# A two-layer cross-attention and mixture-of-experts kernel: where the scatters, the keys, the first maxima and the clears of two tables stand in the order of work

## The chip, the cores and the metric

The program runs on one core of one Trainium2 chip. The metric is the device time of one execution in microseconds. Everything is computed in float32.

Five engines work side by side, each through its own queue of instructions: TensorE (PE, matrix products), VectorE (DVE), ScalarE (ACT), GpSimd (POOL) and SyncE (SP), which issues most of the DMAs. A DMA that goes to places given by a list of indices (a scatter or a gather) is issued by GpSimd.

## The reference

Four blocks are applied to x (4 batches of 512 tokens of 256 numbers). `ctx_1024` is a second input of 4 x 1601 rows.

```python
x = x + L0_xattn(ctx_1024, layernorm(x), ...)   # 8 heads of 128, keys: context and latents
x = x + L0_ffn(layernorm(x), ...)               # 8 experts, top 2, capacity 512
x = x + L1_xattn(ctx_1024, layernorm(x), ...)   # 8 heads of 32, 1601 keys from the context
x = x + L1_ffn(layernorm(x), ...)               # 8 experts, top 2, no capacity
```

In the first expert block every token goes to its two best experts. It gets a slot of the expert in the order of the tokens, and an expert has 512 slots:

```python
slot = where(offsets < capacity, bin_ids * capacity + offsets, E * capacity)
xb   = zeros((E * capacity + 1, hs)).at[slot].set(xf[src])
h    = gelu(einsum('ech,ehf->ecf', xb, w1))
y    = einsum('ecf,efh->ech', h, w2)
out  = zeros((T, hs)).at[src].add(flat_w[order][:, None] * yv)
```

The second attention is a softmax over 1601 keys for each of 8 heads: `softmax(q k^T * scale) v`. The second expert block has no limit to an expert's tokens, and it adds biases.

## The kernel before, in words

The program has four stages, one after the other: first attention (A), first experts (B), second attention (C), second experts (D). A planner in the language's compiler puts the instructions of each engine in order: it follows the program's order where it has a choice, and lets a later instruction go ahead where an earlier one isn't ready by its own reckoning. In some parts the program forbids that: `in_order(*computing)` keeps TensorE, VectorE, ScalarE and GpSimd in the written order (stage C from line 1572 on), and `keep_in_program_order` places one instruction behind the one that was written before it on its engine. SP's queue is not under `in_order` in stage C.

*Stage B.* `route` (three steps: `normalize`, `choose`, `send`) finds the slots of one batch, and `send` (line 308) writes the batch's rows to the DRAM table `slot_x` with 8 scatters. Batches 0 to 2 are routed during stage A, batch 3 in stage B. `all_experts(half, beside)` (line 1222) runs the eight experts on one half of their 512 slots, 256 rows at a time: `fetched` loads the rows from `slot_x` (line 1175) and the expert's two weights of 1 MB each (lines 1178, 1179), `turned` transposes the rows, `hidden` is the first layer with its gelu, `results` the second layer and the store to `slot_y` (line 1220). Row and weight tiles have two buffers each. The first half needs only rows of batches 0 to 2 in the usual case: between the halves, `tc.If(again > 0)` (line 1286) repeats the first half where that did not hold.

`beside` is a generator of other work that is stepped between the experts' pieces, twice for each expert. In the first half it is `keys_first` (line 1258): the routing of batch 3 with its scatters, then 15 steps of keys and values of the second attention for batch 0 (`keys_values`, line 998). In the second half it is `keys_next` (line 1295): the keys and values of batch 1, the collecting of batch 0's results (`add_collected`), its queries, the seven maxima of unit 0 and their way into a row (`negated`, `to_row`).

Also in stage B, four clears are issued with each expert: 8 DMAs fill the second halves of `slot_y` with zeros (line 1248), and 41 DMAs of 530 KB fill the tables `rows_a` and `rows_b` of the second expert block (line 393). Their source `empty` is one row of 265 numbers in each partition.

*Stage C.* The work is cut into 16 units (4 batches x 2 groups of 4 heads x 2 halves of the queries). A unit has 13 steps, one for each block of 128 keys: scores (`weights`, line 1387), exponential (line 1400), sum (line 1409), product with the values (line 1418). The exponential needs the largest score of each query first: `maxima(u, g)` (line 1113, with its reduction on VectorE in line 1124) computes it in 7 pieces, ahead of the unit. `negated` and `to_row` write it into a spare row of `asked`, the tile of the queries, and `keyed`, the tile of the keys, has ones in that row, so that the score comes out less its maximum. `keyed` has one tile for each group of heads. It is filled with zeros and the row of ones (lines 1364, 1365), and `load_keys` (line 1367) brings the keys to their places with 4 DMAs. Both are done at the start of stage C for both tiles, and the first three pieces of unit 1's maxima follow (line 1575). Other work is given a step of the order by `put(step, ...)` (line 1520); the gathers of the next batch's results are put at steps 1 to 8 and their sums at steps 14 to 20, and `load_queries` of unit u at step 13u - 12.

*Stage D* reads `rows_a` and `rows_b`, which the routing in stage C fills.

Of the kernel before, what the change touches and what calls it, by code (L numbers as in the profile page):

```python
# [74 lines left out]
def xattn_ffn_twice(ctx: ExitStack, tc: tile.TileContext, a: dict, out: bass.AP):  # L75
# [267 lines left out]
    def add_collected(b, got, tiles=range(NT)):  # L343
        for t in tiles:
            for k in range(2):
                j = b * NT + t
                xs = x[b][:, t, :]
                nc.vector.scalar_tensor_tensor(
                    xs, got[2 * t + k], prob[k][:, j : j + 1], xs, ALU.mult, ALU.add
                )  # L350
# [31 lines left out]
        nc.sync.dma_start(rbias, a["br"].partition_broadcast(P))  # L382
        nc.sync.dma_start(b2, a["b2"])

    def clear_rows(empty):

        for rows in (rows_a, rows_b):
            n = rows.shape[0]
            for i in range(0, n, 4 * P):
                some = rows[i : min(i + 4 * P, n), :]  # L390

                tc.keep_in_program_order(
                    nc.sync.dma_start(
                        some.rearrange("(p r) d -> p r d", p=P),
                        empty.unsqueeze(1).to_broadcast([P, some.shape[0] // P, PAY]),
                    )
                )
                yield

    def route2(b, two, psum, tag, first=0, n=NT):  # L400

# [651 lines left out]
    for t in shift + asked:  # L1053
        nc.vector.memset(t, 0.0)

    def queries(b, qT):
        xn = soon.tile([P, NT, D], F32, tag="xn", name="xn")
        mv = ln_moments(turns, x[b], NT)
        root = ln_root(turns, mv, NT)
        yield  # L1060
        mv, rs = ln_scale(turns, mv, NT, root)
        for i in range(NT):
            ln_apply(xn, x[b], mv, rs, i)
        yield
        xnT = soon.tile([P, DC, S], F32, tag="xnT", name="xnT")
        transposed(banks["s"], "s", xnT, xn, NT)
        yield
        for o in range(DC):
            ps = banks["s"].tile([P, 512], F32, tag="s", name="ps_q1")
            for c in range(DC):  # L1070
                nc.tensor.matmul(
                    ps,
                    lhsT=wT[:, 0, c, o * P : (o + 1) * P],
                    rhs=xnT[:, c, :],
                    start=c == 0,
                    stop=c == DC - 1,
                )
            nc.scalar.activation(qT[:, o, :], ps, AF.Copy, scale=DH1**-0.5)
            yield

    units = [(b, o, f) for b in range(B) for o in range(DC) for f in range(2)]
    qTs = {}

# [76 lines left out]
    with ExitStack() as st:  # L1160
# [8 lines left out]
        def slots(of, e, half):  # L1169
            s0 = e * CAP + half * HALF  # L1170
            return of[s0 : s0 + HALF, :].rearrange("(t p) d -> p t d", p=P)
# [10 lines left out]
        def turned(e, half, sx, w1, w2):  # L1182
            sxT = two.tile([P, DC, HALF], F32, tag="xT", name="sxT")
            tp = ps_t.tile([P, DC, CT, P], F32, tag="m", name="tp_x")
            for c in range(DC):
                for t in range(CT):
                    nc.tensor.transpose(tp[:, c, t, :], sx[:, t, c * P : (c + 1) * P], ident)
            nc.vector.tensor_copy(sxT, tp.rearrange("p c t q -> p c (t q)"))
            return e, half, sxT, w1, w2
# [32 lines left out]
        def all_experts(half, beside):  # L1222

            here = turned(*fetched(0, half))
            last = None
            for e in range(E):
                done = hidden(*here)
                next(beside, None)
                for _ in range(4):
                    next(clear, None)  # L1230
                if e + 1 < E:
                    here = turned(*fetched(e + 1, half))
                if last:
                    results(*last)
                next(beside, None)
                last = done
            results(*last)
            assert next(beside, None) is None

        empty = rt.tile([P, PAY], F32, name="empty")  # L1240
        nc.gpsimd.memset(empty, 0.0)
        nc.gpsimd.memset(empty[:, D : D + 1], NOWHERE)

        def clears():

            for e in range(E):
                tc.keep_in_program_order(
                    nc.sync.dma_start(
                        slots(slot_y, e, 1), empty[:, :D].unsqueeze(1).to_broadcast([P, CT, D])
                    )  # L1250
                )
                yield
            yield from clear_rows(empty)

        clear = clears()
        kvs = []

        def keys_first():
            normalize()
            yield  # L1260
            choose()
            send()
            yield
            *kv, steps = keys_values(ps_s, "s", 0)
            kvs.append(kv)
            for k, f in enumerate(steps):
                f()
                if k % 2:
                    yield

        normalize, choose, send = route(B - 1, rt, soon, ps_t, "m")
        all_experts(0, keys_first())
# [22 lines left out]
        def keys_next():  # L1295
            *kv, steps = keys_values(ps_s, "s", 1)
            kvs.append(kv)
            for f in steps[:6]:
                f()
            yield  # L1300
            add_collected(0, got0)
            for k, f in enumerate(steps[6:]):
                f()
                if k % 3 == 2:
                    yield
            begin(0)
            for _ in queries(0, qTs[0]):
                yield
            load_queries(0)
            for g in range(len(pieces)):  # L1310
                maxima(0, g)
                yield
            negated(0)
            to_row(0)

        all_experts(1, keys_next())
        assert next(clear, None) is None


    def turned_rows(rows, xT, tp):  # L1320
# [29 lines left out]
    with ExitStack() as st:  # L1350
# [5 lines left out]
        ps_m = st.enter_context(tc.tile_pool(name="c_ps_m", bufs=1, space=PSUM))  # L1356
        banks.update(s=ps_s, m=ps_m)

        keyed = [one.tile([P, 2, M], F32, name=f"keyed{o}") for o in range(DC)]
        of_ones = ones[:, 0:1].to_broadcast([P, M])
        for t in keyed:
            nc.scalar.activation(t[:, 0], of_ones, AF.Copy, scale=in_row[:, 0:1])
            nc.vector.tensor_scalar(t[:, 1], of_ones, in_row[:, 0:1], None, ALU.mult)

        def load_keys(b, o):
            for pair in range(2):
                for s in range(2):
                    i = 2 * pair + s  # L1370
                    nc.sync.dma_start(
                        keyed[o][64 * s : 64 * s + 32, pair, :],
                        kvs[b][0][o][i * DH1 : (i + 1) * DH1, :],
                    )


        by_pool = (1, 4, 7, 10)
# [188 lines left out]

        put(NM * n_units + 2, lambda: first_layer(range(0, FC // 2, 2)))
        put(NM * n_units + 5, lambda: first_layer(range(FC // 2, FC, 2)))

        load_keys(0, 0)  # L1570
        load_keys(0, 1)
        ordered = st.enter_context(in_order(*computing))

        for g in range(3):
            maxima(1, g)
        ahead = {}
        for u in range(1, n_units):
            for g in range(len(pieces)):
# [441 lines left out]
```

## Time and profile before

| | us |
|---|---|
| median of 3 runs | 2905.28 |
| lowest, highest | 2904.32, 2910.24 |
| the profiled execution, its own time | 2910.62 |
| its span, first to last instruction | 2908.8 |
| TensorE busy in the span | 2746.4 (94%) |
| VectorE, ScalarE, GpSimd busy | 1460.5, 935.3, 379.8 |
| TensorE busy, 1546 to 1932 us (stage B and the end of A) | 348.9 of 386 |
| TensorE busy, 1932 to 2604 us (stage C) | 596.0 of 672 |

TensorE is the busiest engine in every stage, so a share below the full one in a stage says how much of that stage is waiting. Busy time in stretches is read with the column of the granted clock beside it (1.00 is the full speed), because a matmul at half clock counts as busy for twice as long. A wait that is named after a DMA was ended by that DMA's landing. SP's queue has no busy time of its own; its lines show when DMAs are issued.

### The profile page before, as it was taken

What the parts mean: (1) busy time and instruction counts of PE and PEld (TensorE: products, weight loads), DVE (VectorE), ACT (ScalarE), POOL (GpSimd) and SP (SyncE); (2) the same over time, 40 slices, a digit from 0 to 9 for tenths busy, and PEclk for the clock granted to TensorE, in tenths of its full rate; (3) what the DMA queues carried; (4) which work ended last, traced back from release to release, by engine and by line L of the source; (5) the groups of instructions that cost most, each with busy time, mean ns of one, the idle gap of its engine ahead of it and who ended that gap; (6) DMA issues with size and microseconds to landing.
All of it is one profiled execution on the core that took longest, in us unless ns stands there. A gap on an engine that the chain in (4) does not pass through costs nothing. (4 is left out here: it accounts for less than half of the span.)

```text
span 2908.8 us, 36010 instructions
## 1 busy us (share of the span) xinstructions
PE 2746.4 (94%) x13614; PEld 1860.1 (64%) x13614; DVE 1460.5 (50%) x2339; ACT 935.3 (32%) x1325; POOL 379.8 (13%) x290
## 2 busy tenths in 40 slices
PE   6999999999999999999998799998989989799998
PEld 2666666766766667666666577864444454458887
DVE  6445556554476444554454302148876767763111
ACT  3323334332343223332332111124434434352221
POOL 0000000100001000000000101002223414152442
PEclk9999999999999999999999999999999999899999
DMA  5444343434344333333335698820001011106563
GB/s 164 111 113 114 97 110 92 109 93 99 89 111 107 97 89 93 97 92 102 95 97 150 197 241 238 236 72 23 23 12 61 24 38 35 39 31 223 161 214 99
DMA packets 196435, 311.96 MB, mean 107 GB/s; under 512 B 43319, under 2 KB 117368, under 8 KB 193560
## 3 DMA queue, kind: packets, MB, share of 16 engines
q1 hardware_dynamic: 157512, 227.52, 29.4%
q0 software_dynamic: 14160, 46.31, 5.4%
q10 hardware_dynamic: 24576, 35.68, 4.8%
q8 instruction: 112, 1.84, 0.3%
q14 instruction: 75, 0.61, 0.1%
HBM read 111.73 MB, written 51.34 MB: 56 GB/s over the span
## 5 line engine op out<-in xcount | busy, mean ns | idle before, releaser
L810 DVE TENSOR_REDUCE top<-ps_s 128x1 f32<-128x2113 f32 x128 | 301.8, 2358 | 581.7 <-PE ps_s L802 581.7
L839 PE MATMUL ps_o<-pT,v 128*128 128x256 f32 x2176 | 521.7, 381 | 0.5 <-DVE inv L817 0.5
L802 PE MATMUL ps_s<-kT,qT 128*128 128x512 f32 (+1 forms) x1280 | 489.0, 526 | 6.0 <-ACT attn L816 6.0
L839 PEld LDWEIGHTS ps_o<-pT,v 128*128 128x128 f32 x2176 | 410.0, 191 | 115.1 <-issue 68.4
L816 ACT ACTIVATE attn<-ps_s,top 128x2113 f32<-128x2113 f32 x128 | 259.0, 2024 | 476.4 <-DVE top L810 446.1
L802 PEld LDWEIGHTS ps_s<-kT,qT 128*128 128x128 f32 x1280 | 241.4, 190 | 252.8 <-issue 236.7
L831 DVE STREAM_TRANSPOSE pT<-swapped 128x2176 f32<-128x2176 f32 x128 | 312.4, 2441 | 33.6 <-DMA swapped<-attn 23.3
L1124 DVE TENSOR_REDUCE tops<-ps_s 128x2 f32<-128x1024 f32 (+1 forms) x224 | 238.0, 1105 | 152.0 <-PE ps_s L1113 151.6
L1387 PE MATMUL ps_w<-asked,keyed 64*128 64x256 f32 (+1 forms) x1664 | 247.4, 420 | 20.3 <-DVE tops L1124 9.5
L751 PE MATMUL ps_k<-kvin,wkv 128*128 128x512 f32 (+1 forms) x640 | 262.7, 533 | 3.3 <-DVE mv_g L689 1.7
L785 PE MATMUL ps_v<-wkv,kvin 128*128 128x256 f32 x1088 | 254.5, 381 | 1.4 <-ACT v L792 1.4
L1387 PEld LDWEIGHTS ps_w<-asked,keyed 64*128 64x128 f32 (+1 forms) x1664 | 149.0, 192 | 147.0 <-ACT pT L1400 61.6
L1400 ACT ACTIVATE pT<-ps_w 128x1024 f32<-128x1024 f32 (+1 forms) x176 | 179.5, 1024 | 195.2 <-PE ps_w L1387 191.8
L785 PEld LDWEIGHTS ps_v<-wkv,kvin 128*128 128x128 f32 x1088 | 204.8, 190 | 36.6 <-ACT v L792 5.9
L1409 DVE TENSOR_TENSOR sum<-sum,pT 128x1024 f32<-128x1024 f32 (+1 forms) x128 | 183.0, 1430 | 10.3 <-ACT pT L1400 4.0
L764 ACT ACTIVATE kT<-ps_k,bqk 128x512 f32<-128x512 f32 (+1 forms) x160 | 96.9, 620 | 266.1 <-PE ps_k L751 123.4
L1409 POOL TENSOR_TENSOR sum<-sum,pT 128x1024 f32<-128x1024 f32 x48 | 122.5, 2553 | 350.3 <-ACT pT L1400 350.1
L751 PEld LDWEIGHTS ps_k<-kvin,wkv 128*128 128x128 f32 x640 | 115.9, 191 | 77.3 <-issue 66.7
L1113 PE MATMUL ps_s<-kv,qT 32*128 32x512 f32 (+1 forms) x1024 | 135.9, 579 | 14.7 <-ACT kv L1017 6.5
L792 ACT COPY v<-ps_v 128x512 f32<-128x512 f32 x144 | 79.9, 561 | 216.7 <-PE ps_v L785 142.1
L1197 PE MATMUL ps_h<-sxT,w 128*128 128x256 f32 x512 | 118.6, 390 | 4.8 <-ACT hT L1204 4.1
L1211 PE MATMUL ps_y<-w,hT 128*128 128x256 f32 x512 | 114.5, 380 | 0.3 <-DVE y L1219 0.2
(300 smaller groups left out, 2662.8 us busy)
## 6 DMA issues: line engine op xcount, KB each, us to landing
swapped<-attn SPq DMA_DIRECT2D x1536, 68.0 KB, 2.0
swapped<-attn ACTq DMA_DIRECT2D x512, 68.0 KB, 2.2
w<-in_w_dram SPq DMA_DIRECT2D x32, 1024.0 KB, 6.2
rows_b<-empty SPq DMA_DIRECT2D x36, 530.0 KB, 14.3
w_e<-in_wall_dram SPq DMA_DIRECT2D x5, 2052.0 KB
cw<-in_ctxT_dram SPq DMA_DIRECT2D x4, 1601.0 KB, 6.4
keyed<-kv SPq DMA_DIRECT2D x32, 200.1 KB, 3.6
ctx_b<-in_ctx_dram SPq DMA_DIRECT2D x3, 1536.0 KB
```

The costliest lines, as they stand in the source:

```text
L751: nc.tensor.matmul(ps[:, :n], lhsT=wkv[:, c, hs], rhs=kvin[:, c, : NB - 1, k, :] if k < 4 else kvin[:, c, NB - 1, :, :], start=c == 0, sto ...
L785: nc.tensor.matmul(ps[:, k, :], lhsT=flat_kvin[c][:, j * P : (j + 1) * P], rhs=wkv[:, c, cols], start=c == 0, stop=c == DC - 1,)
L802: nc.tensor.matmul(flat[:, j0 : j0 + n], lhsT=qT[:, t * P : (t + 1) * P], rhs=kT[:, j0 : j0 + n], start=True, stop=True,)
L810: nc.vector.tensor_reduce(top, flat[:, :L], AX.X, ALU.max, negate=True)
L816: nc.scalar.activation(attn[:, :L], flat[:, :L], AF.Exp, bias=top, accum_out=total)
L831: nc.vector.transpose(pT[:, :, k * P : (k + 1) * P].rearrange("p c (a i) -> p a c i", a=4), swapped.rearrange("p a (c i) -> p a c i", i=32),)
L839: nc.tensor.matmul(ps, lhsT=v[:, j - parts[part][0], (h % 2) * DH0 : (h % 2 + 1) * DH0], rhs=pT[:, j, :], start=j == 0, stop=j == NB - 1,)
L1113: nc.tensor.matmul(pss[i // 2][:, i % 2, at : at + n], lhsT=qTs[b][rows, o, q0 : q0 + P], rhs=kvs[b][0][o][rows, j0 : j0 + n], start=True, ...
L1124: nc.vector.tensor_reduce(tops[u][:, t : t + at // n, 2 * pair : 2 * pair + 2, j0 // 512], of, AX.X, ALU.max,)
L1387: nc.tensor.matmul(ps[:r, s, pair * QH : (pair + 1) * QH], lhsT=keyed[o][64 * s : 64 * s + 64, pair, j * P : j * P + r], rhs=asked[u % 3][ ...
L1400: nc.scalar.activation(pT[:r], ps[:r], AF.Exp)
L1409: (nc.gpsimd if k else nc.vector).tensor_tensor(to, to, pT[:r], ALU.add)
```

## The change

1. `send` (the 8 scatters of batch 3) leaves the second step of `keys_first` and comes at its end, at the 21st call. The steps of keys and values are yielded one by one instead of in pairs, and empty steps are put in up to that call.
2. `beside` is stepped three times for each expert instead of twice.
3. The clears of `slot_y` stand one with each expert of the first half. The 41 clears of the rows leave stage B: each is put at a step of stage C, from step 2 on.
4. The first of the two `keyed` tiles is made in an earlier pool (`soon`), filled in the step of the scatters and loaded in the step after. The second is filled at step 4 of stage C and loaded at step 8. `empty` moves to the pool `soon` as well.
5. The first three pieces of unit 1's maxima move from the start of stage C to the end of `keys_next`, and `to_row(0)` stands after the first of them.

```diff
-    def clear_rows(empty):
+    def clear_rows():
+        def clear(some):
+            tc.keep_in_program_order(
+                nc.sync.dma_start(
+                    some.rearrange("(p r) d -> p r d", p=P),
+                    empty.unsqueeze(1).to_broadcast([P, some.shape[0] // P, PAY]),
+                )
+            )
         for rows in (rows_a, rows_b):
             n = rows.shape[0]
             for i in range(0, n, 4 * P):
...
-                yield
+                yield lambda some=rows[i : min(i + 4 * P, n), :]: clear(some)
...
+    keyed = [soon.tile([P, 2, M], F32, name="keyed0")]
+    def load_keys(b, o):
...
+    def init_keys(t):
+        of_ones = ones[:, 0:1].to_broadcast([P, M])
+        nc.scalar.activation(t[:, 0], of_ones, AF.Copy, scale=in_row[:, 0:1])
+        nc.vector.tensor_scalar(t[:, 1], of_ones, in_row[:, 0:1], None, ALU.mult)
+
+    empty = soon.tile([P, PAY], F32, name="empty")
...
             for e in range(E):
                 done = hidden(*here)
                 next(beside, None)
-                for _ in range(4):
-                    next(clear, None)
+                if half == 0:
+                    clear_results(e)
                 if e + 1 < E:
                     here = turned(*fetched(e + 1, half))
+                next(beside, None)
                 if last:
                     results(*last)
                 next(beside, None)
...
         def keys_first():
             normalize()
             yield
             choose()
-            send()
             yield
             *kv, steps = keys_values(ps_s, "s", 0)
             kvs.append(kv)
-            for k, f in enumerate(steps):
+            for f in steps:
                 f()
-                if k % 2:
-                    yield
+                yield
+            for _ in range(len(steps) + 2, 3 * E - 4):
+                yield
+            send()
+            init_keys(keyed[0])
+            yield
+            load_keys(0, 0)
...
-            for f in steps[:6]:
-                f()
-            yield
-            add_collected(0, got0)
-            for k, f in enumerate(steps[6:]):
+            for k, f in enumerate(steps):
+                if k == 6:
+                    add_collected(0, got0)
                 f()
                 if k % 3 == 2:
                     yield
...
             negated(0)
-            to_row(0)
+            for g in range(3):
+                maxima(1, g)
+                yield
+                if g == 0:
+                    to_row(0)
...
-        keyed = [one.tile([P, 2, M], F32, name=f"keyed{o}") for o in range(DC)]
...
+        keyed.append(one.tile([P, 2, M], F32, name="keyed1"))
...
-        load_keys(0, 0)
-        load_keys(0, 1)
+        for k, f in enumerate(clear_rows()):
+            put(2 + k, f)
+
+        put(4, lambda: init_keys(keyed[1]))
+        put(8, lambda: load_keys(0, 1))
         ordered = st.enter_context(in_order(*computing))
-
-        for g in range(3):
-            maxima(1, g)
```

More of the change, by code (lines that the diff above doesn't have):

```diff
@@ L389, in clear_rows @@
             for i in range(0, n, 4 * P):
[L390 to L397, printed above, removed]
-                yield
+                yield lambda some=rows[i : min(i + 4 * P, n), :]: clear(some)
     def route2(b, two, psum, tag, first=0, n=NT):
@@ L1054, in xattn_ffn_twice @@
         nc.vector.memset(t, 0.0)
+    keyed = [soon.tile([P, 2, M], F32, name="keyed0")]
+    def load_keys(b, o):
+        for pair in range(2):
+            for s in range(2):
+                i = 2 * pair + s
+                nc.sync.dma_start(
+                    keyed[o][64 * s : 64 * s + 32, pair, :],
+                    kvs[b][0][o][i * DH1 : (i + 1) * DH1, :],
+                )
+    def init_keys(t):
[3 more added lines that the diff above has]
+    empty = soon.tile([P, PAY], F32, name="empty")
+    nc.gpsimd.memset(empty, 0.0)
+    nc.gpsimd.memset(empty[:, D : D + 1], NOWHERE)
     def queries(b, qT):
@@ L1079, in queries @@
             yield
+    kvs = []
     units = [(b, o, f) for b in range(B) for o in range(DC) for f in range(2)]
@@ L1238, in all_experts, with clear_results @@
             assert next(beside, None) is None
[L1240 to L1250, printed above, removed]
-                )
-                yield
-            yield from clear_rows(empty)
-        clear = clears()
-        kvs = []
+        def clear_results(e):
+            tc.keep_in_program_order(
+                nc.sync.dma_start(
+                    slots(slot_y, e, 1), empty[:, :D].unsqueeze(1).to_broadcast([P, CT, D])
+                )
+            )
         def keys_first():
@@ L1297, in keys_next @@
             kvs.append(kv)
-            for f in steps[:6]:
-                f()
-            yield
-            add_collected(0, got0)
-            for k, f in enumerate(steps[6:]):
+            for k, f in enumerate(steps):
+                if k == 6:
+                    add_collected(0, got0)
                 f()
@@ L1313, in keys_next @@
             negated(0)
-            to_row(0)
+            for g in range(3):
[3 more added lines that the diff above has]
+                    to_row(0)
         all_experts(1, keys_next())
-        assert next(clear, None) is None
     def turned_rows(rows, xT, tp):
@@ L1357, in xattn_ffn_twice @@
         banks.update(s=ps_s, m=ps_m)
-        keyed = [one.tile([P, 2, M], F32, name=f"keyed{o}") for o in range(DC)]
[L1362 to L1374, printed above, removed]
+        keyed.append(one.tile([P, 2, M], F32, name="keyed1"))
         by_pool = (1, 4, 7, 10)
```

## The prediction

> **What bounds the kernel now.** I read the share of busy time first (TensorE is busy 94% of a 2908.8 us span), then busy time in stretches of 10 us over the stages that the change touches, then the waits there, then the timeline at each hole. TensorE is the bound, so what counts is where it stands still. In the first expert layer (about 1592 to 1932 us) it is nearly always full; this is its one large hole, in busy time by engine (TensorE is the first pair, the granted clock the column after POOL):
>
> ```profile
> 1650.00:1660.00 10.00, 8.02 (x28) 4.34 (x26) 1.88 (x4) 3.05 (x4) 1.44 (x2) 1.00 1.09 278
> 1660.00:1670.00 10.00, 0.00 (x0) 0.00 (x0) 0.00 (x0) 0.00 (x0) 3.46 (x4) 0.57 0.15 47
> 1670.00:1680.00 10.00, 1.12 (x4) 0.72 (x4) 0.44 (x1) 0.00 (x0) 1.96 (x2) 0.50 0.32 107
> 1680.00:1690.00 10.00, 9.69 (x35) 8.13 (x36) 0.26 (x1) 1.79 (x3) 0.00 (x0) 0.74 0.98 291
> 1690.00:1700.00 10.00, 10.00 (x50) 8.52 (x48) 1.38 (x2) 2.99 (x5) 0.00 (x0) 1.00 0.75 215
> ```
>
> From the table of waits (total, times, longest) of 1650 to 1800 us, and of SP's queue:
>
> ```profile
> POOL slot_x L312 <- DMA slot_x<-xn,slot: 27.6, 7, 10.4
> PE tp_x L1187 <- DMA sx<-slot_x: 20.4, 1, 20.4
> ...
> SPq L1175 <- DMA slot_x<-xn,slot: 23.5, 1, 23.5
> ```
>
> The timeline shows the order. The eight scatters of the last batch's rows run one after the other; the loads of the experts' rows, which read the same table, wait for the last:
>
> ```profile
> 1668.19 0.98 POOL L312 DMA_INDIRECT slot_x<-xn,slot  x1 [1.61 <-DMA slot_x<-xn,slot]
> 1670.80 0.98 POOL L312 DMA_INDIRECT slot_x<-xn,slot  x1 [1.62 <-DMA slot_x<-xn,slot]
> 1673.33 0.98 POOL L312 DMA_INDIRECT slot_x<-xn,slot  x1 [1.55 <-DMA slot_x<-xn,slot]
> 1675.71 0.88 SPq L1175 DMA_DIRECT2D sx<-slot_x  x2
> ...
> 1678.41 1.12 PE L1187 MATMUL tp_x<-ident,sx 128*128 128x128 f32 x4 [20.39 <-DMA sx<-slot_x]
> ...
> 1680.31 6.13 PE L1197 MATMUL ps_h<-sxT,w 128*128 128x256 f32 x16 [0.78 <-DVE sxT L1188]
> ```
>
> The second place is the seam to the second attention (timeline, the last expert's matmuls end at 1932.14):
>
> ```profile
> 1932.14 0.60 PE L1146 MATMUL ps_r<-ident,shift 128*128 128x128 f32 x4
> ...
> 1933.99 1.99 PE L1113 MATMUL ps_s<-kv,qT 32*128 32x512 f32 x12 [1.26 <-ACT asked L1150]
> ...
> 1935.61 3.15 ACT L1364 ACTIVATE keyed<-ones,in_row 128x1601 f32<-128x1601 f32 x2 [1.67 <-DMA slot_y<-y]
> 1936.65 5.59 SPq L1371 DMA_DIRECT2D keyed<-kv  x8
> ...
> 1938.73 4.34 PE L1113 MATMUL ps_s<-kv,qT 32*128 32x512 f32 x12 [2.75 <-DVE tops L1124]
> 1943.00 2.08 PE L1387 MATMUL ps_w<-asked,keyed 64*128 64x256 f32 x8
> 1945.01 2.09 PE L1113 MATMUL ps_s<-kv,qT 32*128 32x512 f32 x8
> 1945.19 1.28 ACT L1400 ACT_TABLE_LOAD   x1 [6.43 <-PE ps_w L1387]
> ```
>
> The first weights come 10.9 us after the experts' last matmul: the keys' tile is filled and loaded only there, and the three maxima of unit 1 run there at a halved clock.
>
> **What the Trainium skill says.** "TensorE: Matmul & The Clock Gate" (What's actually happening): an idle window of about 3.4 us halves the clock, a busy one restores it. The trace agrees: 0.50 in 1670 to 1680 us, 1.00 from 1690. "DMA: Bandwidth & Descriptors" (Anatomy of one DMA) puts about 2.0 us of a GpSimd DMA down to set-up and the receipt of the write; here a scatter behind a scatter takes 0.98 us of issue and 1.6 us of waiting, 2.6 in all. The same page (SWDGE vs HWDGE vs iDMA) says that GpSimd's and SP's transfers share 16 engines in turn. The trace agrees: under the clears two scatters waited 10.4 and 8.3 us.
>
> **The change, part by part.** The sum is against the profiled run, 2910.62 us; the runs' median is 2905.28, so 5.3 us come off at the end.
>
> 1. *Scatters behind the first half's loads.* `send` moves to the 21st of the 24 calls, so all eight first-half row loads stand before it. The hole goes: 20.4 us idle, and the cold restart: 16 matmuls took 6.13 us instead of 3.62, four transposes 1.12 instead of 0.60, and 0.8 us of waiting for the eviction. That is 24.2; I take -23.5, since some start-up wait can come back. What is late next? The scatters now need the load for expert 7, which was issued at 1712.2, as soon as expert 5's tile was turned. From there to the second half's first load (1776.3) lie 64 us. The chain costs 3 us of landing and 8 x 2.6 = 21 us on POOL, which has nothing else queued before the gathers at 1774. It is hidden with 40 us to spare. Without that cover it would cost its 21 us.
> 2. *Keys and values of batch 0* are spread over 15 calls instead of being finished by 1658. TensorE does the same work; each expert has about 14.3 us of matmuls, so nothing waits: 0.
> 3. *Clears of the rows* (41 DMAs of 530 KB) leave the experts. There the engines' share was 0.99 (1690 to 1770 us) without one TensorE wait, so the relief is worth nothing in the first half. In the second half the collected rows land up to 8.2 us late instead of 2.8; the moments, the root on ScalarE and the gelu behind it hang on them, and TensorE waits 3.8 us at 1792. Bounds 0 to -3.8; I take -2.
> 4. *Clears in the attention.* The DMA share there is 0.07 (1953 to 2020 us). SP runs ahead of the steps, so it issues them in bursts. Price of one: an expert's 14.3 us held four beside 2 MB of weights. By bytes a clear is 1.8 us, and at most 3.6 if the weights were free. Behind 38 of them stands the query load of unit 4, whose weights come some 162 us into the stage: room for 4.3 us each. Gathers have about 16 us before their sums. So 0, with +4 as the bad end.
> 5. *The seam.* Before: 10.9 us. After: the three maxima (3 x 1.14 = 3.4 us) and the transposes (0.6) are done among the experts, where TensorE is full, so they cost that much there. The first weights follow the experts' last matmul, with perhaps 1.5 us lost while the first exponentials (table load 1.28, then 1.02) free the score buffers. So -10.9 + 3.4 + 0.6 + 1.5 = -5.4. Between 1943 and 1950 the clock was 0.50: 32 matmul records took 8.0 us that take 4.5 at full clock. Some of that is the chain of scores and exponentials anyway: -3. Bounds of both together: -12 and -2.
> 6. *Filling the keys' tiles.* The first (ACT 1.62, DVE 1.05) lies beside experts, where both engines idle. The second moves to step 4 of the attention. VectorE is busy 58.1 of 66.5 us there and every engine follows the written order; queued behind it are exponentials and sums that TensorE waits for. +1.5 (0 to 2.7).
> 7. *Smaller things.* `to_row` now shares its PSUM bank with the experts' transposes, and one ScalarE copy of the keys stands before a gelu: +1 (0 to 3). `empty` now lies in memory that the first attention uses to its end (1609.5); its first reader is a small clear with the planner free to put weight loads ahead. 0, at worst +7, if the next expert's weights queue behind.
>
> Sum: -23.5 - 2 - 5.4 - 3 + 1.5 + 1 = -31.4. Profiled 2879; as a median 2874 us, 1.1% less.
>
> **The rivals.**
> - *A, the forecast: 2874*, own range 2865 to 2884. For it: one wait is named by three views, with long cover in its new place.
> - *B, the seam gives nothing:* the attention's first 70 us hang on VectorE (58 of 66.5 us), so an earlier start only meets its queue earlier. The 8.4 us of step 5 are lost: 2882. Against: VectorE itself waited 2.8 us twice for matmuls in 1943 to 1953.
> - *C, the hole moves, the change not doing what it says:* the planner that orders each engine puts expert 7's load or the scatters so late that the second half's first load waits, or the keys no longer fill TensorE where a weight load is late. Gives back up to the 21 us: 2895. Against: 40 us of slack.
> - *D, slower:* the clears jam SP's queue in the attention. If one takes more than 4.3 us with its rows of 1060 bytes, unit 4's queries and keys come late by 38 times the excess. From (162 + 31) / 38 = 5.1 us each the gain is gone; at 5.5 the stall is 47 us: 2921. For it: a clear's median landing is 14.3 us in the crowded stage. Against: that is queueing, and four fit in 14.3 us.
>
> **How the numbers follow.** A 0.60, B 0.18, C 0.14, D 0.08. The likeliest is 2874. With A's and B's ranges and most of C the range is 2862 to 2896; D lies outside. About 0.2% (6 us) can be told from no change. Faster: A, B and nearly all of C, 0.89; the same, the rest of C and a mild D, 0.04; slower 0.07.
>
> **What would show it.** Right: no wait of the row transposes for `slot_x` above 3 us in the first half; the scatters after the load for expert 7, gone before 40 us from the next load; first weights within 3 us of the experts' last matmul, clock 1.00; the clears in the attention at under 4 us each. Wrong: a new TensorE wait for `sx` or `w` in either half, a wait for `asked` or `keyed` in the first five units, or gathers that keep VectorE waiting.

## The result and the profile after

The changed kernel took 2875.19 us (median of 6 runs, 2865.89 to 2883.17), the kernel before, on the same chip, 2906.35 us (6 runs, 2901.82 to 2913.05). The ratio is 0.9889, with a 95% interval of 0.9868 to 0.9911: between 26 and 38 us less. The forecast was 2874.

The profiled execution took 2883.17 us, with a span of 2881.4. First the stretches in which TensorE stood still before: busy time by engine of the kernel after (TensorE is the first pair, the granted clock the column after POOL, then the DMA share):

```profile
1650.00:1660.00 10.00, 10.00 (x48) 8.80 (x47) 1.39 (x3) 1.20 (x2) 0.00 (x0) 1.00 0.93 307
1660.00:1670.00 10.00, 10.00 (x50) 8.79 (x49) 1.38 (x2) 1.78 (x3) 0.00 (x0) 1.00 0.38 140
1670.00:1680.00 10.00, 10.00 (x48) 8.79 (x47) 0.69 (x1) 1.79 (x4) 0.00 (x0) 1.00 0.50 157
1680.00:1690.00 10.00, 10.00 (x46) 7.84 (x45) 1.11 (x2) 1.78 (x3) 0.99 (x1) 1.00 0.40 141
1690.00:1700.00 10.00, 10.00 (x44) 8.06 (x43) 1.39 (x2) 1.79 (x3) 2.45 (x3) 1.00 0.54 174
```

TensorE is full and at full clock where it had 0.00 and 1.12 us of ten. The table of waits (total, times, longest) of the kernel after, 1650 to 1755 us, has no TensorE wait for `sx`; GpSimd holds it now:

```profile
POOL slot_x L312 <- DMA sx<-slot_x: 61.7, 1, 61.7
...
POOL slot_x L312 <- DMA slot_x<-xn,slot: 22.4, 7, 6.5
...
PE ps_k L1012 <- PEq L1308: 3.0, 1, 3.0
```

The timeline of the kernel after shows the scatters' new place, and the distance to the next reader of their table:

```profile
1688.20 0.99 POOL L312 DMA_INDIRECT slot_x<-xn,slot  x1 [61.71 <-DMA sx<-slot_x]
1691.25 0.99 POOL L312 DMA_INDIRECT slot_x<-xn,slot  x1 [2.06 <-DMA slot_x<-xn,slot]
...
1717.49 0.98 POOL L312 DMA_INDIRECT slot_x<-xn,slot  x1 [6.46 <-DMA slot_x<-xn,slot]
...
1752.39 0.36 SPq L1200 DMA_DIRECT2D sx<-slot_x  x1
...
1910.38 7.17 PE L1236 MATMUL ps_y<-w,hT 128*128 128x256 f32 x32 [0.78 <-DVE y L1244]
...
1918.34 1.14 PE L1395 MATMUL ps_w<-asked,keyed 64*128 64x256 f32 x8 [0.79 <-DVE y L1244]
```

The last scatter is issued at 1717.5, 35 us ahead of the load at 1752.39. Its landing isn't in the trace; the waits of the chain (1.6 to 6.5 us) make it 1720 to 1725 by estimate, some 30 us ahead. From the first issue to the last it is 29.3 us, 4.2 from one to the next. The last expert product ends at 1917.55 and the first weights start 0.8 us later; before, that gap was 10.7 by the same two matmuls.

Where the time went is read best from five boundaries of the timeline: the first matmul of the hidden layer of expert 0; the issue of the second half's first row load; the end of the last expert product; the first weights; the end of the last weights. This table has them for all kernels of the study, in us (one profiled execution each; "first half" to "attention" are the differences, "rest" is what follows):

| kernel | stage A | first half | second half | seam | attention | rest | span |
|---|---|---|---|---|---|---|---|
| before | 1592.4 | 183.9 | 156.0 | 10.7 | 661.1 | 304.7 | 2908.8 |
| after | 1594.9 | 157.5 | 165.2 | 0.8 | 657.1 | 306.0 | 2881.4 |
| after, again | 1592.1 | 157.6 | 163.7 | 0.8 | 656.7 | 303.5 | 2874.3 |
| scatters early | 1593.0 | 175.5 | 165.1 | 0.8 | 653.2 | 299.2 | 2886.8 |
| scatters late only | 1592.4 | 164.6 | 155.9 | 10.7 | 654.2 | 300.9 | 2878.7 |
| clears alone | 1589.0 | 174.8 | 166.0 | 6.7 | 651.1 | 300.5 | 2888.2 |
| maxima in attention | 1595.7 | 157.7 | 172.6 | 6.7 | 656.9 | 305.0 | 2894.5 |
| seam undone | 1595.7 | 157.2 | 172.2 | 6.7 | 654.0 | 305.4 | 2891.3 |
| keys filled by GpSimd | 1593.3 | 157.6 | 173.0 | 0.8 | 649.2 | 306.7 | 2880.5 |
| maxima one by one | 1590.4 | 157.8 | 164.4 | 0.8 | 656.8 | 306.2 | 2876.4 |
| scatters twice | 1591.7 | 157.6 | 163.0 | 0.8 | 652.9 | 300.1 | 2866.2 |
| scatters four times | 1594.0 | 193.5 | 153.0 | 0.8 | 653.6 | 308.2 | 2903.1 |
| clears in experts | 1593.2 | 195.0 | 168.4 | 0.8 | 651.8 | 314.2 | 2923.3 |
| clears twice | 1592.5 | 158.5 | 202.0 | 0.8 | 668.1 | 300.6 | 2922.6 |

The columns differ in worth. The first half repeats within 1.3 us in the eight kernels that should have it alike (157.2 to 157.8, and 158.5 in "clears twice"). The attention and what follows it vary by 7 us and more with the same code (661.1 and 654.2 for `before` and "scatters late only", whose attention is one text), so a few us there are not read as an effect. From before to after, then: -26.4 in the first half, +9.2 in the second, -9.9 in the seam; the other 0.3 us of the 27.4 are the sum of differences (+2.5, -4.0, +1.3) that are within that spread.

The second half got longer by more than the 4 us of work that moved there. Some of the rest is in the maxima themselves. Where two pieces stand side by side around a turned tile, the second takes twice as long. Here is one piece of the kernel before, and one of the two slow ones of the kernel after:

```profile
1882.61 1.14 PE L1113 MATMUL ps_s<-kv,qT 32*128 32x512 f32 x8
```

```profile
1846.76 2.26 PE L1138 MATMUL ps_s<-kv,qT 32*128 32x512 f32 x8 [0.73 <-DVE tops L1149]
```

SP's queue says why the half is no lighter for the clears' going (timeline of the kernel after; `rows_b<-empty` are clears that the change puts at steps of the attention):

```profile
1855.67 9.27 SPq L391 DMA_DIRECT2D rows_b<-empty  x6
1865.04 3.08 SPq L1204 DMA_DIRECT2D w<-in_w_dram  x1
1868.22 5.76 SPq L1245 DMA_DIRECT2D slot_y<-y  x1
1874.03 6.98 SPq L391 DMA_DIRECT2D rows_b<-empty  x4
```

The planner, free to put SP's work earlier, issues 20 of the 41 clears in 1824 to 1881 us, among the second half's experts. Before, 13 stood in that half. The half's DMA share went from 0.68 to 0.77. The attention itself gets the other 21; its burst of 13 took 21.2 us, 1.6 each.

### The profile page after: what moved, and what is told of

It reads as the page before. It is cut to its first block, busy times and chain, and to the rows that moved or that the text cites. A ratio compares the mean times of both kernels' runs of the same rounds, so it can differ in the third digit from the quotient of the medians.

```text
span 2881.4 us, 36020 instructions
## 1 busy us (share of the span) xinstructions
PE 2741.2 (95%) x13614; PEld 1855.3 (64%) x13614; DVE 1455.8 (51%) x2339; ACT 933.6 (32%) x1324; POOL 379.3 (13%) x290
## 5 line engine op out<-in xcount | busy, mean ns | idle before, releaser
L1417 DVE TENSOR_TENSOR sum<-sum,pT 128x1024 f32<-128x1024 f32 (+1 forms) x128 | 177.2, 1385 | 10.7 <-ACT pT L1408 4.4
```

The source lines that it names most:

```text
L1417: (nc.gpsimd if k else nc.vector).tensor_tensor(to, to, pT[:r], ALU.add)
```

## The experiments

Runs of one group are on one chip and share the runs of the kernel before: the first four, the next four, and the last four.

**Scatters early.** The scatters return to the step of the choice; all else is as after.

```diff
             choose()
+            send()
             yield
...
-            send()
             init_keys(keyed[0])
```

> The changed kernel with the eight scatters put back into the second call, everything else as changed (keys spread, clears in the attention, the seam). Theory 1, the place of the scatters is what frees the first half: a wait of the row transposes for slot_x of 15 to 24 us comes back and the time is about 2875 + 24 = 2899 us. Rival, the gain of the first half comes from the keys being spread and the clears being gone (TensorE has filler while it waits, and the chain of scatters runs without traffic): the wait stays under 8 us and the time under 2884 us.

2894.66 us (17 runs), ratio 0.9964 [0.9951, 0.9976]: the scatters' place is worth 16 to 22 us (0.9964 against 0.9908 and 0.9889 for the two measurements of the changed kernel). The hole came back in two parts; TensorE's waits of this kernel, 1640 to 1760 us:

```profile
PE ps_k L1012 <- DMA cw<-in_ctxT_dram: 6.8, 1, 6.8
PE tp_x L1212 <- DMA sx<-slot_x: 5.8, 1, 5.8
```

The time is near theory 1, but the named wait is a third of what that expected. With the clears gone the early chain was faster (its last scatter at 1667.0 us against 1673.3 before), and the planner filled part of the hole with the spread keys, whose own load then came late.

**Scatters late only.** The kernel before, with `send` at the 14th of its 16 calls and nothing else.

```diff
             choose()
-            send()
             yield
...
                 if k % 2:
                     yield
+            for _ in range(9, 13):
+                yield
+            send()
```

> The kernel before with one part of the change only: the scatters at the 14th of the 16 calls, behind the load for expert 7. Theory 1: the 20 us hole goes and nothing else changes, so 2906 - 24 = 2882 us. Rival, the clears that still crowd the DMA engines in the first half stretch the chain of scatters so much (10 us for one, as seen twice before) that the second half's first load waits: 2890 to 2900 us.

2886.52 us (13 runs), ratio 0.9940 [0.9925, 0.9954], some 17 us less than before. No wait for `sx` is left, but the chain ran much longer, and TensorE has another wait at the branch. GpSimd's waits, and then the timeline of this kernel:

```profile
POOL slot_x L312 <- DMA slot_x<-xn,slot: 51.3, 7, 9.0
```

```profile
1694.22 0.99 POOL L312 DMA_INDIRECT slot_x<-xn,slot  x1 [71.27 <-DVE kv L114]
...
1752.38 0.98 POOL L312 DMA_INDIRECT slot_x<-xn,slot  x1 [7.70 <-DMA slot_x<-xn,slot]
...
1755.31 2.79 PE L1010 MATMUL ps_k<-cw 128*128 128x512 f32 x6 [6.39 <-PEq L1288]
```

Beside the clears, seven of the eight scatters waited 7.3 us each for the one ahead: 58 us from the first issue to the last, which left 4.6 us to the second half's first load (1756.98). No TensorE wait for it shows.

TensorE stood 6.4 us at the branch between the halves (PEq is its own sequencer), where the kernels before and after stand 3.0. The chain is not what it waited for. In "scatters four times", below, the chain runs on for 18 us after TensorE has left the branch, and the wait is 3.7. In "clears in experts" the last scatter is issued at 1779.8, TensorE comes to the branch at 1783.3, and the wait is 5.0. What this run and "clears in experts" share is the clears' traffic around the branch: the DMA engines' share during the wait was 0.93 here and 0.62 in "clears in experts", against 0.05 in the kernels before and after and 0.08 in "scatters four times". So the long branch goes with the clears' traffic; why is not shown. The late place is right, and under the clears the chain only just fits there.

**Scatters twice, four times.** The kernel after, with the eight scatters sent two and four times (the same rows to the same places).

```diff
-            send()
+            for _ in range(2):
+                send()
```

> The changed kernel with every scatter of the last batch issued twice (the same rows to the same places). In the changed kernel the chain of eight ran from 1688 to 1720 us and the next load of slot_x stands at 1752, so 32 us are left. Theory, the chain is hidden by this window: sixteen take 42 (at 2.6 us each) to 64 us (at 4 us each) of the 64, the time stays within 5 us of 2875. Rival, the scatters already hold something up (GpSimd's way to the branch, the gathers): plus 20 us or more.

> The same with every scatter issued four times. Theory: 32 scatters take 83 us at 2.6 us each up to 102 at 3.2, the window holds 64, so 19 to 38 us of waiting appear between the halves and the time is 2894 to 2915 us. Rival, there is no such window and the planner would move other work there: under 2885 us.

Twice: 2868.24 us in its one run, first half 157.6, no new wait; sixteen scatters ran from 1684.9 to 1740.1. Four times: 2905.22 us in one run. The last of the 32 was issued at 1784.9, and the reader waited (timeline of this kernel):

```profile
1766.44 5.46 PE L1012 MATMUL ps_k<-cw 128*128 128x512 f32 x6 [3.74 <-PEq L1309]
1790.33 1.09 PE L1212 MATMUL tp_x<-ident,sx 128*128 128x128 f32 x4 [18.44 <-DMA sx<-slot_x]
```

The chain is hidden in the new place, with room for about as much again, and there is an end to it.

**Maxima in attention; seam undone; keys filled by GpSimd.** The first puts the three maxima of unit 1 back at the head of the attention. The second also fills and loads the first keys' tile there. The third keeps all of the change, but fills the second keys' tile by three GpSimd memsets in place of ScalarE and VectorE.

```diff
             negated(0)
-            for g in range(3):
-                maxima(1, g)
-                yield
-                if g == 0:
-                    to_row(0)
+            yield
+            to_row(0)
...
         ordered = st.enter_context(in_order(*computing))
+        for g in range(3):
+            maxima(1, g)
```

In the second also:

```diff
             send()
-            init_keys(keyed[0])
-            yield
-            load_keys(0, 0)
...
+        init_keys(keyed[0])
+        load_keys(0, 0)
         ordered = st.enter_context(in_order(*computing))
```

In the third alone:

```diff
-        put(4, lambda: init_keys(keyed[1]))
+        def init_keys_pool(t):
+            nc.gpsimd.memset(t, 0.0)
+            for r in (32, 96):
+                nc.gpsimd.memset(t[r : r + 1], 1.0)
+        put(4, lambda: init_keys_pool(keyed[1]))
```

> The changed kernel with the first three maxima of unit 1 put back to the head of the second attention (the keys' tile 0 still made early). In the changed kernel the second half of the experts, from its first load to the last product, took 165.0 us against 156.0 before, although only 4.0 us of work were moved there; 5 us of waits for VectorE's reductions and at the last expert came with it. Theory 1, the move gives back what it takes: the head of the attention is 6 to 8 us longer, the experts 8 to 9 us shorter, the time stays within 4 us of 2875. Rival, the forecast's seam (the maxima are cheaper among the experts): plus 5 to 8 us, 2880 to 2883.

> The same, and the keys' tile 0 is filled and loaded at the head of the second attention too, as before. Theory 1: the 10.9 us between the last product of the experts and the first weights come back, the experts take 156 us again: 2875 + 2 = 2877 us. Rival, the forecast: plus 8 us, 2883.

> The changed kernel with the second keys' tile filled at step 4 of the attention by GpSimd (three fills) instead of ScalarE and VectorE. Theory 1, its 1.62 us on ScalarE and 1.05 on VectorE stand in the queues that TensorE waits for: minus 1.5 to 3 us, about 2873. Rival, GpSimd's fills are long (its fill of 265 numbers took 0.33 us, so 3202 take about 4) and hold up its gathers and sums: plus 1 us or more.

Ratios: 0.9919 [0.9905, 0.9934], 0.9927 [0.9912, 0.9941] and 0.9902 [0.9884, 0.9921], six runs each. By time the last can't be told from the kernel after, and I take it as the changed one on this chip. Its trace does tell: the four transposes of unit 1's maxima (`ps_r`) start 26.1 us after the first weights, and 29.3 to 30.2 us after them in ten other kernels that fill this tile in the attention. At the next such transposes it is 61.2 against 62.9 to 64.5. So taking the filling off ScalarE and VectorE gained TensorE 3 to 4 us there, of which about 2 or 3 last, in one execution. That is the theory's mechanism; the time of a whole run doesn't resolve it.

Against the third kernel the first loses 0.17%, the second 0.25%, some 5 and 7 us (8 and 8 between the medians). That is what the rival named, but the intervals overlap, so the loss is likely and not shown. The theories fell in their mechanism: the experts' second half was to get 8 to 9 us shorter, and took 172.6 and 172.2 against 173.0. In the traces the stretch from the second half's first load to the first weights is 173.8 us for the third, 179.3 and 178.9 for the other two: 5.5 and 5.1 longer.

That stretch is 8 us longer on this chip than in the kernel after (166.0). TensorE's waits there, of the three kernels in turn:

```profile
PE ps_h L1222 <- DMA w<-in_w_dram: 6.5, 1, 6.5
...
PE ps_y L1236 <- DMA w<-in_w_dram: 3.1, 1, 3.1
```

```profile
PE ps_h L1222 <- DMA w<-in_w_dram: 5.9, 2, 5.6
...
PE ps_y L1236 <- DMA w<-in_w_dram: 4.8, 1, 4.8
```

```profile
PE ps_h L1222 <- DMA w<-in_w_dram: 5.3, 1, 5.3
```

These are second weights of expert 5 and first weights of expert 7 (counted from 0), which stand in SP's queue behind the clears that the planner put among the experts. A wait also costs something after it: in the third kernel the 32 matmuls behind the 5.3 us took 9.44 us, where in the kernel after they take 7.14. The two together make up most of the 8 us. The DMAs moved 200 GB/s in this half here and 210 in the kernel after; why this chip is slower there stays open. The maxima fill TensorE there and seem to hide part of the lateness: without them 9.6 and 10.7 us of waiting show, with them 5.3, one execution each.

**Clears in experts.** The kernel after, with the 41 clears back in the first layer, four with each expert from the first on, beside the one clear of `slot_y`.

```diff
                 if half == 0:
                     clear_results(e)
+                for _ in range(4):
+                    next(clear, lambda: None)()
...
-        for k, f in enumerate(clear_rows()):
-            put(2 + k, f)
```

> The changed kernel with the 41 clears of the rows back among the experts, four with each. Run 2 showed the chain of eight scatters under the clears' traffic at 7 us each, about 60 us instead of 32. Theory 1, the clears matter because they stretch this chain to the edge of its window: it ends within 5 us of the branch or after it, TensorE waits 3 to 8 us longer there, 2879 to 2883 us. Rival, the forecast's step 3, where only the gathers behind the branch gain: plus 2 us, 2877.

2927.2 us (6 runs), ratio 1.0046 [1.0032, 1.0061]: slower than before, and both expectations missed by some 40 us. From the timeline of this kernel:

```profile
1622.18 13.18 SPq L391 DMA_DIRECT2D rows_b<-empty  x4
1635.47 2.32 SPq L1204 DMA_DIRECT2D w<-in_w_dram  x1
...
1645.35 6.68 SPq L391 DMA_DIRECT2D rows_b<-empty  x4
1652.07 2.29 SPq L1203 DMA_DIRECT2D w<-in_w_dram  x1
...
1668.40 8.82 PE L1222 MATMUL ps_h<-sxT,w 128*128 128x256 f32 x32 [8.01 <-DMA w<-in_w_dram]
...
1776.43 6.82 PE L1012 MATMUL ps_k<-cw 128*128 128x512 f32 x10 [8.32 <-DMA cw<-in_ctxT_dram]
...
1788.21 2.79 PE L1012 MATMUL ps_k<-cw 128*128 128x512 f32 x6 [4.96 <-PEq L1312]
```

Four clears held SP's queue for 13 us with a weight load behind them, the next four for 7 with the load (at 1652.07) that TensorE then waits 8 us for, and TensorE ran dry several times. This is not the kernel before with late scatters, though: it issues 44 clears in the first half where before issued 36, and large ones from expert 0 on, where before issued only the small ones of `slot_y` with the first two; its keys are spread as well. It shows that this many clears are too much for that half, not what the move of the clears was worth. Which of these differences makes the 31 us between it and "scatters late only" (by the ratios) was not tried.

**Clears alone.** For that worth: seam undone, with the scatters early as well, so that of the change the move of the clears, the spread keys and the third call are left. (`to_row` keeps its place beside an expert, so its seam is 6.7 us and not 10.7.)

```diff
             choose()
+            send()
             yield
...
-            send()
-            init_keys(keyed[0])
-            yield
-            load_keys(0, 0)
```

> The clears of the second layer's tables stay in attention and the keys stay spread, but the scatters follow the choice again and the keys' second tile, the first maxima and their load stand at the head of stage C again: the move of the clears alone. Forecast's steps (3 and 4 together -2, with the hole in TensorE left as it was): 2900 to 2906, ratio 0.998 to 1.000. Theory from the run with the clears put back among the experts (they are worth some 45 us only where the scatters already lie behind the first half's loads, so that the hole no longer drains the queue): the same 0.997 to 1.000, since here the hole is there; the two moves would then be worth far more together than the sum of each alone. Rival (the clears cost the experts' stage tens of us whatever the order of the scatters): 2860 to 2885, ratio 0.984 to 0.993.

2899.54 us (22 runs), ratio 0.9984 [0.9974, 0.9994]: 4.6 us less than before (2 to 8). From the timeline of this kernel:

```profile
1659.77 2.05 PE L1012 MATMUL ps_k<-cw 128*128 128x512 f32 x2 [6.96 <-DMA cw<-in_ctxT_dram]
...
1667.37 1.12 PE L1212 MATMUL tp_x<-ident,sx 128*128 128x128 f32 x4 [5.56 <-DMA sx<-slot_x]
...
1906.14 8.83 PE L1222 MATMUL ps_h<-sxT,w 128*128 128x256 f32 x32 [4.46 <-DMA w<-in_w_dram]
```

The first half is 9.1 us shorter although the scatters are early: the hole shrank to 12.5 us. The second half is 10 us longer with no maxima moved into it; 4.5 of them wait for weights behind clears. The seam is 4.0 shorter by the place of `to_row`, so the 4.6 us are not the clears' alone: in this trace what they give in the first half is gone in the second. The two moves nearly add up: in the first half -19.3 (scatters alone) and -9.1 (this kernel) against -26.4 together. My idea after the run before, that the clears cost tens of us once the hole is gone and nothing while it is there, fell: the ratios of scatters alone (0.9940) and of clears and scatters with the seam undone (0.9927) lie 0.13% apart, about 4 us, and this kernel's 0.9984 gives as little.

**After again, maxima one by one.** The changed kernel once more, as the measure on this chip, and a version meant to beat it: no two pieces of the maxima side by side around the turned rows, and one left for the last expert.

```diff
-            for g in range(len(pieces)):
-                maxima(0, g)
-                yield
-            negated(0)
-            for g in range(3):
-                maxima(1, g)
-                yield
-                if g == 0:
-                    to_row(0)
+            call = 11
+            for u, g in [(0, g) for g in range(len(pieces))] + [(1, g) for g in range(3)]:
+                if call > 12 and call % 3 == 2:
+                    yield
+                    call += 1
+                maxima(u, g)
+                if (u, g) == (0, len(pieces) - 1):
+                    negated(0)
+                if (u, g) == (1, 0):
+                    to_row(0)
+                yield
+                call += 1
```

> The changed kernel itself once more, on the chip of these runs, as the measure for the others: ratio to before 0.987 to 0.991.

> As the changed kernel, but no two pieces of the maxima stand side by side around a turned tile: ten pieces go to the places after the hidden layer and after the results of experts 3 to 7, none between, so that the last y eviction has a piece beside it too, and the row's transposes come after the last turned tile. Theory (the second half's waits for VectorE's maxima, for the shared bank's copies and for the last y eviction, 0.3 to 0.8 us each, 3 to 4.5 us in all, are what keep the seam from giving its full forecast): those waits go from the trace and the time falls by 2 to 4 us against the changed kernel on the same chip (ratio between the two 0.9986 to 0.9993, hardly above what the rounds can tell). Rival (the granted clock takes back what the waits give): the waits go and the second half's stretch is no shorter, 0 to -1 us.

0.9908 [0.9894, 0.9922] and 0.9890 [0.9876, 0.9905], four runs each: 2877.36 and 2875.78 us, not told apart. TensorE's waits in the second half, first of the changed kernel run again, then of the new version:

```profile
PE ps_h L1222 <- ACT hT L1229: 2.8, 1, 2.8
PE ps_s L1138 <- DVE tops L1149: 1.8, 3, 0.7
PE ps_y L1236 <- DVE y L1244: 0.8, 1, 0.8
PE ps_h L1222 <- DMA w<-in_w_dram: 0.6, 1, 0.6
PE tp_x L1212 <- ACT asked L1175: 0.4, 1, 0.4
```

```profile
PE ps_h L1222 <- ACT hT L1229: 5.7, 1, 5.7
...
PE ps_y L1236 <- DMA w<-in_w_dram: 1.7, 1, 1.7
PE ps_h L1222 <- DMA w<-in_w_dram: 1.4, 1, 1.4
```

The aimed-at waits went, 3.0 us in all. 2.5 us came back at the weights of experts 6 and 7, and the wait behind the collected rows, which the edit does not touch, was 2.9 us longer in this execution. The half is 164.4 us against 163.7. The slow pieces of the maxima went too (none takes 2.26 us). Neither expectation names what took the gain back: it was the next late transfers. The granted clock was lower too, 0.97 in this half against 0.98; whether it took a part or only follows from the new waits can't be told here.

**Clears twice.** Every clear is issued twice.

```diff
-            put(2 + k, f)
+            put(2 + k, f, f)
```

> Every clear of the second layer's tables is issued twice in attention, 82 instead of 41, with the same contents. Theory (each costs SP's queue 1.6 to 2.1 us behind which only loads with time to spare stand; 82 take 131 to 172 us against some 162 us of room): hidden or nearly, 0 to +6 us, 2865 to 2890. Rival D of the forecast (SP's queue is nearly jammed by 38 clears, and TensorE soon waits for the rows of asked or keyed): a wait of 10 us or more shows on the first weights of a unit and the time is 2895 or more.

2924.32 us in one run, 47 more than the changed kernel's median on this chip. From its timeline, and then what SP's queue waited for from 1907.46 to 1935.72 us, the time of its first row:

```profile
1907.48 28.24 SPq L391 DMA_DIRECT2D rows_b<-empty  x9
1935.76 0.63 SPq L1204 DMA_DIRECT2D w<-in_w_dram  x1
...
1944.35 8.74 PE L1236 MATMUL ps_y<-w,hT 128*128 128x256 f32 x32 [25.59 <-DMA w<-in_w_dram]
...
1960.00 6.92 SPq L391 DMA_DIRECT2D rows_b<-empty  x3
1967.03 0.57 SPq L1245 DMA_DIRECT2D slot_y<-y  x1
1971.30 1.28 ACT L1408 ACT_TABLE_LOAD   x1 [68.76 <-DMA slot_y<-y]
...
1973.67 1.65 PE L1395 MATMUL ps_w<-asked,keyed 64*128 64x256 f32 x6 [15.09 <-ACT sum L1408]
```

```profile
SPq L391 <- DMA rows_b<-empty: 22.6, 4, 6.2
```

Rival D's number came, but the run doesn't show its mechanism. The second copy of a clear writes the rows of the first, and SP waits until that has landed: 22.6 of the 28.24 us of the nine clears are four such waits. The changed kernel has one wait of a clear for a clear, of 3.6 us (1815 to 1985 us). So the doubling brought in a dependency of its own. What 82 clears of different rows would cost stays open, and my theory of the room with it. What the run does show is who stands behind the clears when SP's queue is held. It is not the query load of unit 4. It is the last experts' second weights, since the clears are put ahead of their steps, and then the last experts' store, for which the first exponential waits.

## Why the prediction was right, and where its terms were not

The sum was -31.4 us for the profiled execution and for the median; the medians moved by 31.2 on the first chip, and the ratio of the repeat, 0.9908, makes it 27. The size is right, and so is the place of the largest term. That the sum fits this closely is partly luck: in the traces the first half gave more than its term, and the second half with the seam much less (0.7 us instead of 5.4 and 2).

1. *Scatters, -23.5.* Right in place and mechanism: the first half lost 26.4 us, no wait of the turned rows for `sx` is left, and with the scatters early 18 us of the first half return. Mis-sized: a scatter behind a scatter costs 4.2 us and not 2.6, so some 30 us were spare and not 40. By itself the move gives 19.3 us in the first half: under the old clears the chain ran 58 us, TensorE stood 6.4 us at the branch instead of 3.0, and waited 1.6 for a weight load of expert 7.
2. *Keys spread, 0.* Not tried apart from the clears. With early scatters they filled part of the hole.
3. *Clears leave the experts, -2.* Wrong in both halves, right by luck in its sum. "Worth nothing in the first half": with the spread keys it gave 9.1 us there alone, and 7.1 beside late scatters (164.6 to 157.5), with the early chain faster in the first case (a wait of 5.6 us for `sx` instead of 20.4, of 7.0 for the contexts beside it) and the branch and a weight load quicker in the second (5.0 of the 7.1). (The Trainium skill, "DMA: Bandwidth & Descriptors", SWDGE vs HWDGE vs iDMA, has GpSimd's and SP's transfers take turns on the same 16 engines; the waits of a chained scatter, 7.3 us beside the clears and 3.2 without, fit that.) "Late collected rows in the second half": the wait behind them went only from 3.8 to 3.3 us, and the planner issues 20 clears in that half where 13 stood. Together 4.6 us, measured with 4.0 of the seam in it.
4. *Clears in the attention, 0, bad end +4.* No wait for `asked` or `keyed` shows, and a burst costs 1.6 us each. "SP runs ahead of the steps" was written and not followed to its end: ahead meant into the experts. The cost there, 0 to 5.3 us of waiting for weights with the change in full, depends on the execution and the chip. With every clear twice it is 33.5 us, behind clears that wait for their first copies.
5. *The seam, -5.4, and its cold clock, -3.* The gap closed as forecast, from 10.7 to 0.8 us. The forecast's 4 us of moved work were 9.2 in the second half. Besides that work, waits grew by 2.2 us: new ones for VectorE's maxima where two pieces are adjacent (1.7), for the bank that `to_row` shares (0.4) and for a y eviction (0.8), less what went elsewhere. The maxima themselves took some 3 us more: two pieces 2.26 us instead of 1.14, and less in two others. "Maxima one by one", where no two pieces are adjacent, has none of these waits and no piece of 2.26. From the second half's first load to the first weights only 0.7 us were won in the first trace, 2.2 in the repeat. Against the seam undone on the same chip it is 5 to 7 us, with the cover that the maxima give to late weights in it. The cold clock went as forecast (0.50 in 1943 to 1950 us before, 1.00 in the first 7 us of weights after; the first eight take 1.14 us instead of 2.08). Whether that is worth 3 us in the total can't be seen: the attention varies by more.
6. *Filling the second keys' tile, +1.5*, and 7. *bank and `empty`, +1.* The first is mis-sized by its trace: without it TensorE is 3 to 4 us further at the first later mark and 2 to 3 at the next, in one execution. The bank's copy cost 0.4 us, and `empty`, cleared at 1615 instead of 1329, held nothing up.

Of the rivals, B (the seam gives nothing) is not excluded by the first trace alone, and is made unlikely by the two undone seams. C did not come. D did not come with 41 clears: they took 1.6 us each in the attention's burst, against its limit of 4.3. Its victim was the wrong one, as the waits for weights show; its mechanism was not tried without the second copies' own waits.

Left open: 41 clears put some twenty steps later, beyond the planner's reach of the last experts. The waits for `w` point to it, and it was not tried.

## What to carry to other kernels

A chain of dependent small transfers is best put behind its table's last reader, but price it under the traffic of its new place: the same eight scatters took 29 us from the first issue to the last beside weight loads and 58 beside clears as well. When work is moved to a later stage through a planner that may hoist it, find in the trace where it was issued, because the queue ahead of the stage pays for it. When two edits act on the same wait, run each alone: the sum of a forecast can be right with its terms wrong. And when a run doubles some work to price it, look for waits of the second copy for the first, as they are not in the kernel that is to be priced.

## What the runs showed of the hardware that was not expected

- A scatter that waits for the one ahead costs, issue included, 3.2 us (32 in a row), 4.2 (eight beside weight loads) or 8.3 (eight beside weights and clears, 7.3 of it waiting).
- A clear of 530 KB occupies SP's queue for 1.6 us in the attention's burst (21.2 us for 13), and for 1.1 to 3.3 beside weight loads (4.35 to 13.18 us for four in "clears in experts"); what stands behind it in the queue is issued that much later.
- TensorE stands 2.9 to 3.7 us at the branch between the halves in twelve kernels, and 6.4 and 5.0 in the two where clears' traffic goes on during it (DMA share 0.93 and 0.62).
- Nearly the same attention code took 649 to 657 us in the changed kernels at granted clocks of 0.94 to 0.96, the shortest (649.2) where GpSimd fills the second keys' tile. The rest of that spread has no cause shown here.
